# A first pair of sequences with a stream of its own: loads in order of use, offset sums on VectorE, second places for q and k, pinned orders

## The chip, the cores and the metric

One core of a Trainium2 chip. The metric is device microseconds of one execution; smaller is better. All times below are microseconds (us) unless marked otherwise, counted in the profile from the start of the span.

## The reference

Two transformer layers over x of shape (16, 256, 512) with a context of the same shape, 16 heads of 32.

```python
# layer 0: cross attention with a mask, then a GELU MLP
xq, ctx = layer_norm(x, qn_w, qn_b), layer_norm(context, cn_w, cn_b)
q, (k, v) = xq @ q_w, split(ctx @ kv_w)
attn = softmax(where(xa_mask, -max, q @ k.T / sqrt(32)))
x = x + (attn @ v) @ proj_w + proj_b
x = x + gelu(layer_norm(x, n2_w, n2_b) @ fc1_w + fc1_b) @ fc2_w + fc2_b
# layer 1: causal self attention, cross attention, a ReLU MLP, each with a residual and a layer norm
```

The change is in the start of layer 0's attention.

## The kernel before

The 16 sequences are taken as 8 pairs (`NB = 2`, `NG = 8`); a pair has 512 rows, `G = 4` tiles of 128. Matrix products run in float32r, and each operand is held as a high part and a rest, so a product is three matrix instructions (`mm3`).

`phase1` is layer 0's attention. For each pair, `feed(g)` makes the inputs of attention: `normal` loads a tile of x or of the context and normalises it (statistics on VectorE, a power on GpSimd, scaling on VectorE); `transposed` turns it on TensorE and `split` writes high part (ScalarE) and rest (VectorE) into `x_t` or `c_t`; `project_t` makes q and k, four column blocks each with 12 instructions of 512 columns; `values` makes v. `att.stream` is the attention itself: scores (`ps_s`), mask and minimum, exponential, transposes, product with v.

The norms' gain and offset are folded into the weights. `Weight.load` fetches a 128x512 piece into a staging tile `wst` and writes gain times piece, high part on ScalarE (L193) and rest on VectorE (L194). `weigh` (from L216) sums offset times piece over the four pieces into `by_k`: the first on GpSimd (L220), the others scaled on ScalarE (L222) and added on GpSimd (L223). `shift` makes the bias from that sum with matrix products against ones (`ps_b`, L230) and copies it (L231). The splits of q and k (L122, L123) need this bias. `load_o` does the same for the output weight, whose offset is v's bias.

`att.keep` stores a q or k tile to DRAM scratch (`d<-qk`), and `build` loads head stacks from there (`stack<-d`). There is one place for a q tile and one for a k tile (`halves`, `bufs=1`), so a split waits for the store before it.

`weave` interleaves attention with `feed`. In the first round attention only marks its start, so `feed(0)` runs alone: the first scores come when all of it has been put on TensorE. After that `feed(1)` and later ones run beside the attention of the pair before.

TensorE's instructions keep the program's order (`manual_schedule` on PE). For ScalarE, VectorE, GpSimd and SyncE (which issues all transfers) a planner chooses the order, by simulated costs, when the program is built; on the chip each engine then runs its list in order.

Of the kernel before, what the change touches and what calls it, by code (L numbers as in the profile page):

```python
# [2 lines left out]

# [7 lines left out]
F32 = mybir.dt.float32  # L11
# [30 lines left out]
def kernel(ctx: ExitStack, tc: tile.TileContext, a, out):  # L42
# [72 lines left out]
    def bcast(dram_row, n):  # L115
        return dram_row.to_broadcast([P, n])


    def split(src, dst, bias=None, scale=None):

        if bias is not None:
            nc.scalar.activation(dst[0], src, AF.Identity, bias=bias)  # L122
            nc.vector.scalar_tensor_tensor(  # L123
                dst[1], src, bias, dst[0].bitcast(F32), ALU.add, ALU.subtract
            )
        elif scale is not None:
            nc.scalar.activation(dst[0], src, AF.Copy, scale=scale)
            nc.vector.scalar_tensor_tensor(  # L128
                dst[1], src, scale, dst[0].bitcast(F32), ALU.mult, ALU.subtract
            )  # L130
        else:
            nc.scalar.copy(dst[0], src)
            nc.vector.tensor_tensor(dst[1], src, dst[0].bitcast(F32), ALU.subtract)

    def split_sb(src, dst):
        nc.vector.tensor_copy(dst[0], src)
# [7 lines left out]
    class Weight:  # L144
# [29 lines left out]

        def load(self, ks, x0=0, n=C):

            at = slice(x0, x0 + n)
            for k in ks:
                h, l = self.w[0][:, k, at], self.w[1][:, k, at]
                raw = self.stage()  # L180
                nc.sync.dma_start(
                    out=raw, in_=a[self.name][ts(k, P), self.c0 + x0 : self.c0 + x0 + n]
                )
                self.raw[k] = raw
                if self.gain is None:
                    if self.pooled:
                        nc.gpsimd.tensor_copy(h, raw)
                    else:
                        nc.scalar.copy(h, raw)
                    nc.gpsimd.tensor_tensor(out=l, in0=raw, in1=h.bitcast(F32), op=ALU.subtract)  # L190
                else:
                    by = self.gain[:, k : k + 1]
                    nc.scalar.activation(h, raw, AF.Identity, scale=by)  # L193
                    nc.vector.scalar_tensor_tensor(  # L194
                        l, raw, by, h.bitcast(F32), ALU.mult, ALU.subtract
                    )
        def weigh(self, pool):

            self.by_k = None
            for k, raw in self.raw.items():  # L200
                self.by_k = weigh(pool, self.by_k, raw, self.offset[:, k : k + 1])

        def shift(self):
            by_k = self.by_k
# [8 lines left out]
        w.load(range(KC))  # L213
        return w

    def weigh(pool, total, raw, offset):  # L216

        if total is None:
            total = pool.tile([P, 512], F32, tag="xr", name="by_k", bufs=3)
            nc.gpsimd.tensor_scalar(total, raw, offset, None, ALU.mult)  # L220
        else:
            nc.scalar.activation(raw, raw, AF.Identity, scale=offset)  # L222
            nc.gpsimd.tensor_tensor(out=total, in0=total, in1=raw, op=ALU.add)  # L223
        return total

    def sum_cols(b, by_k):

        ps = bank("mm", "ps_b")
        for c in range(4):
            nc.tensor.matmul(ps[:, c : c + 1], by_k[:, ts(c, P)], ones, start=True, stop=True)  # L230
        nc.vector.tensor_copy(b, ps[:, 0:4])  # L231
# [312 lines left out]
    def values(pool, w, src, v, tiles, between=()):  # L544
        for t in tiles:
            ps = yield from project(w, src, t)
            vt = pool.tile([P, C], F32, tag="v", name="v", bufs=6)
            nc.scalar.copy(vt, ps)
            v.append(vt)
            if t - tiles[0] < len(between):  # L550
                yield between[t - tiles[0]]()


    def phase1():
# [7 lines left out]
        att = Attention(pool, scratch, 3, False)  # L562
        w = {}

        def stage():
            return pool.tile([P, C], F32, tag="pts", name="wst", bufs=6)

        def load(n):
            by, off = (cvec[:, x, :] for x in ((0, 1) if n == "q" else (2, 3)))
            w[n] = load_weight(  # L570
                wqkv,
                stage,
                "q_w" if n == "q" else "kv_w",
                KC,
                C,
                C if n == "v" else 0,
                by,
                off,
                "col",
                wo,  # L580
            )
            w[n].weigh(wo)

        def load_o():
            w["o"] = load_weight(wo, stage, "proj_w", KC, C, form="row")
            w["b_o"] = wo.tile([P, C], F32, name="b_o")
            nc.sync.dma_start(out=w["b_o"], in_=bcast(a["proj_b"], C))

            w["o"].offset = w["v"].b
            w["o"].weigh(wo)  # L590
# [5 lines left out]
        class Block0(Job):  # L596
# [5 lines left out]
                    self.shared = (HPC - 1,)  # L602

            def begin(self):
                if self.g == 0:
                    self.load_mask()
                    for t in range(G):
                        self.mask(t)
                if self.g + 1 < NG:
                    after = jobs[self.g + 1]  # L610
                    after.load_mask()
                    att.later += [lambda t=t: after.mask(t) for t in range(G)]
# [38 lines left out]
        jobs = [Block0(g) for g in range(NG)]  # L651
        inputs = {}

        def normal(g, tag, t):
            x = ins.tile([P, C], F32, tag="xin", name="xin", bufs=4)
            nc.sync.dma_start(out=x, in_=of({"x_t": "x", "c_t": "ctx"}[tag], g)[:, t, :])
            normalize(pool, x, x)
            return x

        def front(g, tag, t, x=None):  # L660
            def go():
# [6 lines left out]
        def residual_row(g, at, xr=None):  # L668
            if xr is None:
                xr = wo.tile([P, C], F32, tag="xr", name="xr", bufs=3)  # L670
            nc.sync.dma_start(out=xr, in_=of("x", g)[:, at, :])
            nc.gpsimd.tensor_tensor(out=xr, in0=xr, in1=w["b_o"], op=ALU.add)
            return xr

        def turned(n):
            while att.done < n * KC:
                yield None

        def residual(g, i, xrs=None):
            yield from turned(g * NB + i + 1)  # L680
            for t in range(NT):
# [3 lines left out]
                nc.vector.tensor_tensor(xr, ps, xr, ALU.add)  # L685
                nc.sync.dma_start(out=xd[0][g][ts(at, P), :], in_=xr)

        def feed(g):
            if g >= 1:
                yield from more_values(g - 1)  # L690
            if g >= 2:
                yield from residual(g - 2, 1)
            if g < NG:
                job = jobs[g]
                if g == 0:
                    ready = [normal(g, "x_t", t) for t in range(G)]
                    nc.sync.dma_start(out=cvec, in_=a["attn_vec"])
                    nc.sync.dma_start(out=n2, in_=a["mlp_vec"])
                    nc.sync.dma_start(out=b_fc1, in_=a["fc1_b"])
                    load("q")  # L700
                    for t in range(G):
                        yield front(g, "x_t", t, ready[t])()
                for c in range(KC):
                    ps = yield from project_t(w["q"].w, c, inputs["x_t"])
                    if g == 0 and c == 0:
                        w["q"].shift()
                    q, hl = halves(ins, 0)
                    split(ps, hl, w["q"].b[:, c : c + 1])
                    att.keep(job, c, 0, q)
                    for t in FRONTS[c]:  # L710
                        yield front(g, "c_t", t)()
                if g == 1:
                    shift_o()
                if g == 0:
                    load("k")
                for c in range(KC):
                    ps = yield from project_t(w["k"].w, c, inputs["c_t"])
                    if g == 0 and c == 0:
                        w["k"].shift()
                    k, hl = halves(ins, 1)  # L720
                    split(ps, hl, w["k"].b[:, c : c + 1])
                    att.keep(job, c, 1, k)
                    if g + 1 < NG:
                        for t in FRONTS[c]:
                            yield front(g + 1, "x_t", t)()
                if g == 0:
                    load("v")
                yield from values(pool, w["v"].w, inputs["c_t"], job.v, range(NT))
                if g == 0:
                    w["v"].shift()  # L730
                    load_o()
            if g >= 1:
                yield from residual(g - 1, 0)

        def more_values(g):

# [15 lines left out]

        main = att.stream(jobs)
        for r in range(NG):
            weave(main, Attention.COST, feed(r), (16 * 12 + 8) * PASS)
        weave(main, Attention.COST, last(), (6 * 12 + 32) * PASS)
        left.close()
        return w["mlp"]
# [869 lines left out]
```

## Time and profile before

| | |
|---|---|
| median of 3 runs | 2765.36 us (2759.3 to 2766.42) |
| the profiled execution | 2762.91 us, its span 2761.2 us |
| TensorE busy | 2657.0 us (96%) |
| VectorE busy | 2051.9 us (74%) |
| ScalarE busy | 1821.9 us (66%) |
| GpSimd busy | 630.3 us (23%) |
| first scores product on TensorE | 70.25 us |

Busy times of different engines overlap. Where an engine is named PE, PEld, DVE, ACT, POOL or SP, it is TensorE's products, its weight loads, VectorE, ScalarE, GpSimd or SyncE. In a list of waits the columns are: who waited, for whom, total us, times, longest. In a list of groups they are: line, engine, operation, output from inputs, shapes and count, then busy us and mean ns of one, then the idle time before them. The granted clock is TensorE's, 1.00 at full speed; the record has no entry before its first change, and reads 1.00 there.

### The profile page before, as it was taken

Reading aid. Unit: us, or ns where it says so; the run is one execution under the profiler, and the core shown is the slowest. Engines: PE = TensorE matmul, PEld = TensorE weight load, DVE = VectorE, ACT = ScalarE, POOL = GpSimd, SP = SyncE. Lnnn points to the kernel's source line nnn. Section 1 sums busy time; section 2 is a strip of 40 time slices with the busy share of each in tenths; the row PEclk is TensorE's granted clock in tenths of the full one; section 3 lists DMA queues with packets and bytes.
Section 4 is the critical chain, followed back from the end, with each engine's and each line's share of the span. In section 5 each row is a group of like instructions: output and inputs, shape, how many; then the busy total and the mean of one; then the engine's idle time right before and its main releaser. Section 6 shows DMA issues by size and latency. Waiting matters only on the chain.

```text
span 2761.2 us, 56625 instructions
## 1 busy us (share of the span) xinstructions
PE 2657.0 (96%) x18970; PEld 2241.7 (81%) x18970; DVE 2051.9 (74%) x5947; ACT 1821.9 (66%) x5286; POOL 630.3 (23%) x696
## 2 busy tenths in 40 slices
PE   6999999999899998999989999999999999999998
PEld 5777777776899998999968777777777777777787
DVE  7766667657955569999957777777777777777887
ACT  4877777777655555444547778786777776777522
POOL 6222212113401100111211111115212221214333
PEclk9999999999999999999999999999999999999999
DMA  6655656656333344443464665667565665655321
GB/s 214 197 183 170 182 171 192 182 164 169 107 123 138 123 150 175 168 157 136 167 225 159 195 197 187 194 190 227 183 196 188 188 194 170 189 174 173 97 91 54
DMA packets 287808, 465.40 MB, mean 169 GB/s; under 512 B 36256, under 2 KB 188320, under 8 KB 279328
## 3 DMA queue, kind: packets, MB, share of 16 engines
q1 hardware_dynamic: 287520, 461.78, 52.0%
q8 instruction: 153, 2.51, 0.4%
q14 instruction: 135, 1.11, 0.1%
HBM read 284.97 MB, written 176.69 MB: 167 GB/s over the span
## 4 chain that ended last, share of the span: by engine, by line
PE 76%; DVE 10%; DMA 4%; ACT 3%; issue 3%; POOL 2%; SPq 1%; POOLq 0%; DVEq 0%; ACTq 0%
PE ps_p L258 18%; PE ps_v L258 14%; PE down L1027 9%; PE ps_pt L449 9%; PE ps_z L468 5%; PE ps_s L408 5%; PE up_sc L914 5%; PE up_pt L914 3%; PE up_mm L914 3%; PE ps_t L277 2%; DVE e L423 1%; ACT e L433 1%; DVE x L252 1%; DMA d<-qk 1%; PE ps_z L1347 1%
## 5 line engine op out<-in xcount | busy, mean ns | idle before, releaser
L433 ACT ACTIVATE e<-e,mn 128x256 f32<-128x256 f32 (+1 forms) x1024 | 487.5, 480 | 71.7 <-DVE mn L423 69.4
L455 ACT COPY pt<-ps_pt 128x512 f32<-128x512 f32 (+1 forms) x696 | 378.3, 546 | 178.5 <-PE ps_pt L449 165.5
L449 PE MATMUL ps_pt<-ident,e 128*128 128x128 f32 x2816 | 436.3, 273 | 15.4 <-DVE lbias L1289 8.8
L449 PEld LDWEIGHTS ps_pt<-ident,e 128*128 128x128 f32 x2816 | 336.3, 140 | 56.3 <-DVE lbias L1289 5.7
L408 PE MATMUL ps_s<-stack 97*128 97x256 f32 (+1 forms) x1536 | 331.8, 297 | 18.8 <-ACT e L433 12.0
L408 PEld LDWEIGHTS ps_s<-stack 97*128 97x128 f32 (+1 forms) x1536 | 269.0, 190 | 78.3 <-ACT e L433 19.2
L433 ACT ACTIVATE e<-ps_s,mn 128x256 f32<-128x256 f32 x512 | 240.9, 483 | 59.2 <-DVE mn L419 44.0
L1356 POOL TENSOR_TENSOR x<-x,zz 128x256 f32<-128x256 f32 x128 | 95.4, 745 | 737.0 <-DVE zz L1349 687.0
L1027 PE MATMUL down<-w_h,c_t 128*128 128x256 f32 x900 | 255.4, 285 | 5.6 <-DVE c_t L142 5.6
L1027 PE MATMUL down<-w_h,x_t 128*128 128x256 f32 x868 | 245.9, 283 | 4.4 <-ACT x_t L141 4.4
L423 DVE CUSTOM_DVE_ANT_0 e<-mb,ps_s 128x256 f32<-128x256 bf16 x512 | 192.7, 415 | 75.4 <-PE ps_s L408 73.8
L1027 PE MATMUL down<-w_l,x_t 128*128 128x256 f32 x868 | 246.2, 284 | 0.0
L242 POOL TENSOR_TENSOR rstd<-rstd,nhalf 128x1 f32<-128x1 f32 x192 | 142.4, 747 | 360.6 <-DVE rstd L241 358.8
L258 PE MATMUL ps_p<-x_t,q_h 128*128 128x512 f32 x640 | 215.4, 417 | 4.2 <-DVE qk L128 2.1
L419 DVE TENSOR_REDUCE mn<-ps_s 128x2 f32<-128x512 f32 x256 | 175.1, 684 | 48.7 <-PE ps_s L408 46.5
L468 PE MATMUL ps_z<-pt,v 128*32 128x256 f32 (+1 forms) x3072 | 202.2, 370 | 7.2 <-DVE pt L453 6.5
L423 DVE CUSTOM_DVE_ANT_0 e<-tri,ps_s 128x128 f32<-128x128 f32 (+1 forms) x512 | 160.2, 346 | 53.6 <-PE ps_s L408 51.3
L433 ACT ACTIVATION_READ_ACCUMULATOR e<-e,mn 128x1 f32 x1024 | 197.5, 193 | 0.0
L1027 PEld LDWEIGHTS down<-w_h,c_t 128*128 128x128 f32 x900 | 171.0, 190 | 7.8 <-DVE c_t L142 7.8
L1027 PEld LDWEIGHTS down<-w_h,x_t 128*128 128x128 f32 x868 | 166.4, 192 | 4.8 <-ACT x_t L141 4.6
L468 PEld LDWEIGHTS ps_z<-pt,v 128*32 128x32 f32 x3072 | 83.5, 109 | 105.8 <-issue 28.0
L1027 PEld LDWEIGHTS down<-w_l,x_t 128*128 128x128 f32 x868 | 165.2, 190 | 0.0
(250 smaller groups left out, 7247.8 us busy)
## 6 DMA issues: line engine op xcount, KB each, us to landing
stack<-d SPq DMA_DIRECT2D x1152, 128.0 KB
d<-qk SPq DMA_DIRECT2D x192, 512.0 KB
hid<-ho SPq DMA_DIRECT2D x32, 1024.0 KB
raw<-hid SPq DMA_DIRECT2D x32, 1024.0 KB
x<-xd SPq DMA_DIRECT2D x128, 256.0 KB
xd<-x SPq DMA_DIRECT2D x96, 256.0 KB
xin<-in_x_dram SPq DMA_DIRECT2D x32, 256.0 KB
xin<-in_ctx_dram SPq DMA_DIRECT2D x32, 256.0 KB
```

Source lines behind the costliest of these rows:

```text
L242: nc.gpsimd.tensor_tensor(out=rstd[:, 1:2], in0=rstd[:, 0:1], in1=nhalf, op=ALU.pow)
L258: nc.tensor.matmul(ps, w[p], x[q], start=(k == 0 and i == 0), stop=(k == kc - 1 and i == 2))
L408: nc.tensor.matmul(ps[:, t, :], u.st[: self.rows, 0, j, ts(t, P)], u.st[: self.rows, 1, j, :], start=True, stop=True,)
L419: nc.vector.tensor_reduce(mn, ps, AX.X, ALU.min)
L423: nc.vector.tensor_tensor_reduce(out=e[:, at], in0=bias[t], in1=ps[:, t, : job.width[t]], scale=-SC, scalar=BIG, op0=ALU.add, op1=ALU.min, ...
L433: nc.scalar.activation(e[:, at], ps[:, t, :] if bias is None else e[:, at], AF.Exp, bias=mn[:, t : t + 1], scale=-1.0, accum_out=u.rs[:, t ...
L449: nc.tensor.transpose(pp[:, ts(x, P)], e[:, at : at + P], ident)
L455: nc.scalar.copy(pt[:, :n], pp[:, :n])
L468: nc.tensor.matmul(z[ts(j, D), w[0] * P :], job.v[u.i * NT + mc][:, u.c * P + j * D : u.c * P + (j + 1) * D], u.pt[j][:, x0 * P : (x0 + le ...
L914: nc.tensor.matmul(ps[:, mm, :], w[p][:, k, :], x[q][:, k, :], start=(first and mm == k == j == 0), stop=(k == 1 and j == 2), skip_group_c ...
L1027: nc.tensor.matmul(ps[:, t, :], x[p][:, mm, ts(t, P)], w[r][:, bo, :], start=(q == mm == t == j == 0), stop=(q == self.NS - 1 and mm == 1 ...
L1356: nc.gpsimd.tensor_tensor(out=xv, in0=xv, in1=zz, op=ALU.add)
```

## The change

The first pair leaves `feed` and gets `first()`, woven in the same place.

- `first_loads` issues, as one block in program order on SyncE: x of the first pair, the norm vectors, q's pieces, the context, k's pieces, three of v's, the mask, x of the second pair, v's fourth piece. `Weight.load` is divided into `fetch` and `part`. Staging takes the 6 places of `pts` and, for five pieces, those of the exponentials `e`; the context is loaded into places of v.
- 40 transposes of the identity with itself are put on TensorE ahead, and 5 after each x tile; nothing reads them.
- `weigh` runs on VectorE: one `tensor_scalar` and three `scalar_tensor_tensor`, each multiply and add. This holds for the output weight too.
- Column blocks 1 to 3 of q and k of the first pair are written to places of `z_t` instead of the single q or k place.
- `behind(...)` pins what a block issues on an engine behind a given instruction of that engine.
- The first mask is converted on ScalarE, after k's last split; the output weight is loaded and converted behind v's copies; `n2` and `b_fc1` are loaded there too. The bias product uses a `pt` bank in place of an `mm` bank. Residual rows of pair 0 keep the program's order.

```diff
+        def fetch(self, k, x0=0, n=C):
+            self.raw[k] = self.stage()
+            nc.sync.dma_start(
+                out=self.raw[k], in_=a[self.name][ts(k, P), self.c0 + x0 : self.c0 + x0 + n]
+            )
+        def part(self, k, x0=0, n=C):
...
+                by = self.gain[:, k : k + 1]
+                nc.scalar.activation(h, raw, AF.Identity, scale=by)
+                latest["w"] = nc.vector.scalar_tensor_tensor(
+                    l, raw, by, h.bitcast(F32), ALU.mult, ALU.subtract
                 )
+        def weigh(self, pool):
+            self.by_k = pool.tile([P, 512], F32, tag="xr", name="by_k", bufs=3)
+            for k, raw in self.raw.items():
+                by = self.offset[:, k : k + 1]
+                if k == 0:
+                    nc.vector.tensor_scalar(self.by_k, raw, by, None, ALU.mult)
                 else:
+                    last = nc.vector.scalar_tensor_tensor(
+                        self.by_k, raw, by, self.by_k, ALU.mult, ALU.add
                     )
+            return last
...
-        if total is None:
-            total = pool.tile([P, 512], F32, tag="xr", name="by_k", bufs=3)
-            nc.gpsimd.tensor_scalar(total, raw, offset, None, ALU.mult)
-        else:
-            nc.scalar.activation(raw, raw, AF.Identity, scale=offset)
-            nc.gpsimd.tensor_tensor(out=total, in0=total, in1=raw, op=ALU.add)
...
-        ps = bank("mm", "ps_b")
+        ps = bank("pt", "ps_b")
...
+        def behind(those):
+            with ExitStack() as stack:
+                for x in those:
+                    stack.enter_context(tc.issue_after(x))
+                yield
+        places = iter([("pts", 6)] * 6 + [("e", 5)] * 5)
...
+            nc.sync.dma_start(out=n2, in_=a["mlp_vec"])
+            nc.sync.dma_start(out=b_fc1, in_=a["fc1_b"])
...
+        def first_loads():
+            for t in range(G):
+                fetched[0, "x_t", t] = fetch(0, "x_t", t)
+            nc.sync.dma_start(out=cvec, in_=a["attn_vec"])
+            for n in "qkv":
+                weight(n)
+            for k in range(KC):
+                w["q"].fetch(k)
+            for t in range(G):
+                fetched[0, "c_t", t] = fetch(0, "c_t", t)
+            for n in "kv":
+                for k in range(KC):
+                    if n == "k" or k < 3:
+                        w[n].fetch(k)
+            jobs[0].load_mask()
+            for t in range(G):
+                fetched[1, "x_t", t] = fetch(1, "x_t", t)
+            w["v"].fetch(3)
...
+            if g == 0:
+                tc.keep_in_program_order(load)
...
+        turns = itertools.cycle((0, 1))
+        def spare_halves(slot):
+            tag = f"z_t{next(turns)}"
+            t = wo.tile([P, KC, S], F32R, tag=tag, name=f"qk{slot}", bufs=2)
...
+        def first():
+            job = jobs[0]
+            idle = bank("z", "ps_w")
+            def turn_nothing(n):
+                for i in range(n):
+                    nc.tensor.transpose(idle[:, ts(i % KC, P)], ident, ident)
+            turn_nothing(40)
+            with tc.manual_schedule(engines={mybir.EngineType.SP}):
+                first_loads()
+            ready = [normal(0, "x_t", t) for t in range(G)]
+            w["q"].part(0)
+            for t in range(G):
+                yield front(0, "x_t", t, ready[t])()
+                turn_nothing(5)
+            with behind((latest["h"].ins, latest["l"].ins)):
+                for k in range(1, KC):
+                    w["q"].part(k)
+            inputs_split, q_rest = latest["h"].ins, latest["w"].ins
+            with behind((q_rest,)):
+                w["q"].weigh(wo)
+            def keep(n, slot, c, ps):
+                t, hl = (spare_halves if c else lambda slot: halves(ins, slot))(slot)
+                split(ps, hl, w[n].b[:, c : c + 1])
+                att.keep(job, c, slot, t)
+            for c in range(KC):
+                ps = yield from project_t(w["q"].w, c, inputs["x_t"])
+                if c == 0:
+                    ps0 = ps
+                    continue
+                if c == 1:
+                    w["q"].shift()
+                    keep("q", 0, 0, ps0)
+                keep("q", 0, c, ps)
+                if c == 1:
+                    with behind((inputs_split, latest["l"].ins)):
+                        load("k")
+                for t in ((), (), (0, 1, 2), (3,))[c]:
+                    with behind((q_rest,)):
+                        cost = front(0, "c_t", t)()
+                    yield cost
+            context_split = latest["h"].ins, latest["l"].ins
+            with behind(context_split):
+                k_sum = w["k"].weigh(wo).ins
+            for c in range(KC):
+                ps = yield from project_t(w["k"].w, c, inputs["c_t"])
+                if c == 0:
+                    w["k"].shift()
+                    with behind((context_split[0], k_sum)):
+                        load("v")
+                keep("k", 1, c, ps)
+                for t in FRONTS[c]:
+                    with behind(context_split[1:]):
+                        cost = front(1, "x_t", t)()
+                    yield cost
+            with behind((latest["l"].ins,)):
+                w["v"].weigh(wo)
+            yield from values(pool, w["v"].w, inputs["c_t"], job.v, range(NT))
+            with behind((latest["h"].ins,)):
+                for t in range(G):
+                    nc.scalar.activation(job.mb[:, t, :], job.mk[:, t, :], AF.Copy, scale=NEG)
+                w["v"].shift()
+            with behind((latest["v"].ins,)):
+                load_o()
...
-            weave(main, Attention.COST, feed(r), (16 * 12 + 8) * PASS)
+            weave(main, Attention.COST, feed(r) if r else first(), (16 * 12 + 8) * PASS)
```

## The prediction

> **What bounds the kernel now.** The page comes first: TensorE is busy 2657.0 us of 2761.2, so any time in which it has nothing to run is lost from the end. I then asked for the busy time by stretch, cut where the first pair of sequences starts and stops. The first scores matrix product starts at 70.25 (timeline). Columns: length, then busy time (count) of PE, PEld, DVE, ACT and POOL, granted clock, DMA share, GB/s.
>
> ```profile
> 0.00:7.66 7.66, 0.00 (x0) 0.00 (x0) 3.63 (x12) 1.49 (x2) 3.92 (x21) 1.00 0.74 214
> 7.66:19.07 11.41, 4.97 (x17) 3.29 (x17) 10.71 (x22) 9.50 (x16) 10.51 (x9) 1.00 0.86 283
> 19.07:31.13 12.06, 8.62 (x27) 6.51 (x28) 9.75 (x19) 7.00 (x12) 11.71 (x11) 0.81 0.34 103
> 31.13:45.85 14.72, 13.42 (x56) 10.42 (x56) 9.60 (x18) 4.21 (x8) 13.32 (x14) 0.92 0.70 228
> 45.85:52.48 6.63, 2.70 (x17) 2.10 (x17) 4.67 (x9) 3.04 (x5) 1.83 (x2) 0.85 0.45 159
> 52.48:70.25 17.77, 17.77 (x77) 14.56 (x76) 10.66 (x24) 4.77 (x8) 2.19 (x4) 0.86 0.74 254
> ```
>
> PE works 47.47 of these 70.25 us, VectorE 49.02, GpSimd 43.47. After 70.25 PE is busy 2609.51 of 2690.92 (97%). PE's order is written by hand and does not change after the first pair, so I take it that a first scores product that is G us earlier ends the kernel G us earlier. T is the time of that product, 70.25 now. Next, PE's waits before T:
>
> ```profile
> PE ps_t L277 <- DVE xin L247: 11.3, 4, 7.7
> PE ps_b L230 <- POOL by_k L223: 3.2, 1, 3.2
> PE ps_p L258 <- DVE x_t L133: 2.9, 1, 2.9
> PE ps_b L230 <- DVE qk L123: 1.9, 1, 1.9
> ```
>
> The first is mostly the load of x (7.7); the others are the offset sums on GpSimd and VectorE working on other things first. The chain of waits adds a transfer and shows matrix products at two speeds:
>
> ```profile
> 39.51 6.51 DMA d<-qk
> 46.11 0.70 ACT qk L122
> ...
> 52.69 5.04 PE ps_p L258 x12
> ...
> 64.19 5.44 PE ps_v L258 x24
> ```
>
> There is one place for q, so the next split waits for the store. Twelve products take 5.04 at the half clock (0.42 each), 24 take 5.44 at the full one (0.227). Last, the prices (groups before 70.3):
>
> ```profile
> L223 POOL TENSOR_TENSOR by_k<-by_k,wst 128x512 f32<-128x512 f32 x9 | 12.2, 1361 | 0.2
> L247 DVE TENSOR_SCALAR xin<-xin,mv,rstd 128x512 f32<-128x512 f32 x16 | 11.9, 751 | 1.5 <-POOL rstd L242 1.4
> L194 DVE SCALAR_TENSOR_TENSOR kv_w_l<-wst,cvec,kv_w_h 128x512 fp32r<-128x512 f32 x8 | 8.9, 1124 | 1.6 <-ACT kv_w_h L193 1.6
> L194 DVE SCALAR_TENSOR_TENSOR q_w_l<-wst,cvec,q_w_h 128x512 fp32r<-128x512 f32 x4 | 3.0, 743 | 0.7 <-ACT q_w_h L193 0.7
> ```
>
> The same L194 instruction costs 0.743 for q and 1.124 for k and v, and L247 varies from 0.54 to 1.54, where GpSimd runs offset sums and mask conversions beside it.
>
> **The floor of the new start.** PE: 120 products x 0.227 = 27.2, 12 x 4 transposes x 0.11 = 5.3 (the chain has four in 0.44), three bias products x 0.9 = 2.7: 35.2, after x at 7.7. VectorE: 12 normalisations x 1.43 (0.69 + 0.10 + 0.10 + 0.54, by start times) = 17.2; 12 weight parts x 0.743 = 8.9; 12 splits x 0.68 = 8.2; 8 q/k splits x 0.75 = 6.0; and the offset sums that come to it, 3 x (0.53 + 3 x 0.74) = 8.3. Together 48.6 from 3.5 on. The scale-only step takes 0.53 as L247 does alone; the multiply-add has two SBUF inputs as L194 has, so 0.74 and at worst 1.12. No row has that operation on VectorE; the worst adds 9 x 0.38 = 3.4, and below 0.53 nothing speaks for a gain. So VectorE is the tight engine, and no T under 53 is to be had.
>
> **Part by part, along VectorE and PE.**
>
> *Loads.* Five of SP's issue groups are put in one order: about 29 issues of 0.4 us, 6.6 MB. At the 283 GB/s of the second stretch that is 23 us: q by 8 to 10, context by 15, k by 19, v by 22. None is used earlier than that. Two of them wait in SP's queue, the next pair's x for places that x frees (12 to 18), v's last piece for q's first raw piece (after q's sum, 18). Behind them stand the stores of q, which start at 21 at the earliest: cost 0; without that cover each us would delay stack loads that have some 25 us of slack before T.
>
> *Idle transposes.* 40 start at 1.75, when the identity is ready (POOL, 1.41 + 0.29). At the half clock one takes 0.22 (eight in 1.97), at the full one 0.11. PE's clock changes in steps of 3.41 us in this trace (to half at 26.58, full at 33.41, half at 50.48, full at 57.31). On that grid one step ends at 6.1, so 20 run slowly, 20 fast, and they end at 8.3, when x is there. The last x tile is transposed by 11.8, 4 x 5 idle ones between; its split ends at 13.2.
>
> *q.* Its other three parts are pinned behind that split; VectorE ends the last at 15.5, PE's first column block at 16.1, the second at 18.9. The sum runs 15.5 to 18.2, so the bias product (18.9 to 19.9) no longer waits, which removes the 3.2. The split places remove the 6.51 store from the chain; six of the eight q and k tiles get spare ones.
>
> *Context.* The four normalisations follow the q sum: VectorE has 5.7 for them, 3.0 for q splits, 2.7 for context splits, 3.0 for k parts, 14.4 from 18.2: last context split at 32.5, since k parts and q splits share the queue. PE would be ready at 30: a new wait of 2.5, VectorE's.
>
> *k.* First block 32.5 to 35.3; k's sum is pinned behind the context splits and ends at 36.0; bias 37.0. Then v's parts (3.0) stand ahead of the next pair's x normalisations in program order, so PE, which wants their transposes next, gets the first at 41.5: a wait of 4.5 that the change makes. From there three blocks 8.3, four sets of transposes 1.8 with 2.2 of waits for their normalisations, v's two blocks 5.5, v's bias 1.0: T = 41.5 + 18.8 = 60.3. If the planner places part of the normalisations ahead of v's parts, 2 us less. I take **T = 59.3**, G = 11.0.
>
> *After T.* Mask conversion on ScalarE: 4 x 0.48 (nearest row: L433, 128x256), beside v's products: 0. The output weight's conversion moves behind v's copies, 4 x 0.61 = 2.45 on ScalarE's queue, ahead of exponentials; the three L222 at 70.71 (1.95) are gone: +0.5. Its sum, 2.8 on VectorE, where 70.25 to 80 has 5.59 of 9.75 busy: hidden, 2.8 if not.
>
> Sum: -11.0 + 0.5 = -10.5. The profiled execution took 2762.91 (span 2761.2), so 2752.4; the median shown is 2.45 above it, so 2754.9. A measurement here tells 0.3% from nothing, 8.3 us.
>
> **Does an idle transpose raise the clock?** These stretches are the clock's own steps:
>
> ```profile
> 26.58:30.00 3.42, 3.08 (x13) 2.68 (x14) 2.19 (x4) 1.71 (x4) 3.21 (x4) 0.50 0.20 79
> 30.00:33.41 3.41, 3.14 (x9) 2.28 (x9) 1.78 (x3) 2.55 (x5) 3.27 (x5) 0.50 0.58 172
> 50.48:53.90 3.42, 2.69 (x10) 1.89 (x9) 2.98 (x5) 2.00 (x4) 0.10 (x1) 0.50 0.41 126
> ```
>
> The first, 90% busy with bias products and transposes, did not bring the full clock; the second, 0.86 of transposes and the rest wide products, did; the third, 1.48 of transposes and 1.4 of products, did not. No step here is filled by transposes alone, so it stays open. The Trainium skill, "TensorE: Matmul & The Clock Gate", Part 4: PE-mode transpose, says that transposes do not count as busy for the clock, which speaks against this part. By that rule the first row is as it should be, and the sum would be that of the first rival.
>
> **Rivals.**
>
> 1. *The clock stays at half through the transposes.* 40 x 0.215 = 8.6 end at 10.4; four sets of nine at 1.93 end at 18.1; the last split at 18.3 instead of 13.2, and all that is pinned behind it 5 later. T = 64.3, gain 5.5: 2759.9, no difference. For it the row at 26.58; against it that wide products could be what lacked there. 0.20.
>
> 2. *VectorE's pinned queue has holes.* T = 3.5 + 48.6/u + 1.0 at a busy share u. T = 59.3 needs 0.89. VectorE's share from 3.5 to 70.25 is 0.73 now; at that T = 71, time 2767, no difference. It turns slower below 0.66. Against it: the waits in those stretches are for GpSimd, stores and loads, which the change takes away. 0.04 within 0.3%, 0.04 slower.
>
> 3. *The rest is planned anew, for the worse.* ScalarE, VectorE, GpSimd and SP run in an order that a planner lays out from its own costs, and the start feeds into it. PE idles 81.4 us after T, in places such as 2.54 at 658.7 behind VectorE's pt. If that grows by over 18.8 us (23%) the kernel is slower; at 25%, +20.4, 2775.3. Against it: neighbouring 100 us stretches of one kind differ by under 2 us. Slower, 0.08.
>
> 4. *The planner fills the two new waits* (2.5 and 4.5), T = 53 to 54, VectorE's floor: gain up to 16.5, 2749. Against it: no stretch above has VectorE without holes. 0.10.
>
> **How the numbers follow.** The forecast, 2754.9, has 0.54. Faster: 0.54 + 0.10 = 0.64; same: 0.20 + 0.04 = 0.24; slower: 0.04 + 0.08 = 0.12. The range goes down to 2745.5, rival 4 less 3.5 us of spread between executions (the runs shown lie up to 6.1 under their median), and up to 2767, which takes in rival 1 and the no-gain end of rival 2; the slower cases, 0.12, are left out. The forecast's own range is 2750 to 2757.
>
> **What would show it.** The first scores product near 59; wide products at 0.23 from the first on (right) or transposes at 0.22 to 12 and beyond (rival 1); the q bias product with no wait for the sum; PE's waits before T led by VectorE's normalisations near 25 to 32 and 37 to 42; no wait of the q and k splits (L122 now) for d<-qk. PE's idle time after T, 81.4 now, would show rival 3. The prediction is wrong if T falls by 9 or more and the end does not.

## The result, and the profile after

The changed kernel takes 2742.9 us (median of 6 runs, 2737.32 to 2745.44), the kernel before 2763.47 (6 runs, 2759.3 to 2767.84): a ratio of 0.9921 [0.9907, 0.9936], 20.6 us less. The forecast was 2754.9 with a range from 2745.5; the gain was nearly twice the 10.5 forecast, and the time lies 2.6 us below the range. The profiled execution took 2743.56 us, its span is 2741.8.

T, the start of the first scores product, went from 70.25 to 62.71: a gain of 7.5, where 11.0 was forecast. The other 12 us came after T, where the sum had a loss of 0.5. The busy time by stretch after the change (columns as before: length, busy time and count of PE, PEld, DVE, ACT and POOL, granted clock, DMA share, GB/s):

```profile
0.00:7.66 7.66, 5.92 (x40) 5.74 (x40) 3.53 (x11) 1.49 (x2) 3.91 (x21) 1.00 0.72 236
...
25.10:38.80 13.70, 9.27 (x45) 6.72 (x43) 11.15 (x23) 5.85 (x10) 1.09 (x2) 1.00 0.73 240
38.80:49.04 10.24, 8.22 (x26) 6.82 (x27) 8.96 (x24) 1.75 (x3) 2.33 (x4) 0.50 0.32 103
49.04:62.71 13.67, 13.39 (x67) 10.89 (x66) 9.45 (x18) 5.98 (x13) 1.10 (x2) 1.00 0.69 233
62.71:2741.80 2679.09, 2607.86 (x18780) 2206.26 (x18779) 2001.46 (x5852) 1793.37 (x5237) 590.31 (x641) 0.99 0.53 168
```

Read the last row first. PE does the same 18,780 products as before after T, with 1.65 us less busy time (2607.86 against 2609.51), but it is idle for 71.2 us there instead of 81.4. This idle time was the sign that the prediction named for its third rival; it moved the other way. The row from 38.80 holds a surprise of the start: the granted clock is half for 10.24 us.

PE's waits before T in the changed kernel (who waited, for whom, total, times, longest):

```profile
PE ps_b L236 <- DVE by_k L214: 4.0, 3, 2.2
...
PE ps_t L283 <- DVE xin L253: 1.2, 1, 1.2
```

The 11.3 us for normalised tiles fell to 1.2, the 3.2 for GpSimd's sums are gone; what leads now are the bias products, which wait for VectorE's sums (1.5 for q, 2.2 for k). The prices of VectorE in the start (groups of instructions: busy us and mean ns of one, then idle time before):

```profile
L214 DVE SCALAR_TENSOR_TENSOR by_k<-wst,cvec,by_k 128x512 f32<-128x512 f32 x9 | 6.6, 737 | 0.1
L253 DVE TENSOR_SCALAR xin<-xin,mv,rstd 128x512 f32<-128x512 f32 x12 | 6.4, 537 | 1.8 <-POOL rstd L248 1.7
L202 DVE SCALAR_TENSOR_TENSOR kv_w_l<-wst,cvec,kv_w_h 128x512 fp32r<-128x512 f32 x8 | 5.5, 744 | 0.0
```

An add is 0.737, a weight part of k and v 0.744 (1.124 before), a scaling 0.537 (0.751 before): every one costs about what its cheapest row of before cost. The waits after T show where part of the 12 us was; this line of the kernel before

```profile
PE ps_s L408 <- ACT e L433: 12.0, 16, 3.0
```

has become, in the changed kernel,

```profile
PE ps_s L414 <- ACT e L439: 6.6, 15, 0.7
```

No such wait is longer than 0.7 in this profile. (In a second profile of each kernel it is 15.5 with a longest of 3.2 before, and 10.4 with a longest of 1.5 after.) Yet from 165 us on ScalarE, GpSimd and SP run the same lists in the same order in both kernels, and VectorE too but for one exchange near 1080 us: hardly anything was planned anew there.

### The profile page after: what moved, and what is told of

Read it like the earlier page. It is cut to its first block, busy times and chain, and to the rows that moved or that the text cites. A ratio compares the mean times of both kernels' runs of the same rounds, so it can differ in the third digit from the quotient of the medians.

```text
span 2741.8 us, 56705 instructions
## 1 busy us (share of the span) xinstructions
PE 2659.8 (97%) x19030; PEld 2248.4 (82%) x19030; DVE 2050.6 (75%) x5963; ACT 1817.0 (66%) x5278; POOL 602.3 (22%) x676
## 3 DMA queue, kind: packets, MB, share of 16 engines
q8 instruction: 153, 2.51, 0.4%
## 4 chain that ended last, share of the span: by engine, by line
PE 77%; DVE 11%; DMA 5%; issue 3%; ACT 2%; POOL 1%; SPq 1%; POOLq 0%; DVEq 0%; ACTq 0%
PE ps_p L264 18%; PE ps_v L264 14%; PE down L1138 10%; PE ps_pt L455 9%; PE ps_s L414 5%; PE ps_z L474 5%; PE up_sc L1025 5%; PE up_pt L1025 3%; PE up_mm L1025 3%; PE ps_t L283 2%; DMA d<-qk 1%; DVE e L429 1%; ACT e L439 1%; DVE x L258 1%; DVE st L244 1%
## 5 line engine op out<-in xcount | busy, mean ns | idle before, releaser
L414 PE MATMUL ps_s<-stack 97*128 97x256 f32 (+1 forms) x1536 | 332.6, 298 | 13.1 <-ACT e L439 6.6
```

What stands on the lines that cost most here:

```text
L414: nc.tensor.matmul(ps[:, t, :], u.st[: self.rows, 0, j, ts(t, P)], u.st[: self.rows, 1, j, :], start=True, stop=True,)
```

## The experiments

Twelve kernels ran, four at a time; each batch has its own runs of the kernel before on the same chip (medians 2769.69, 2763.81, 2769.28), so ratios are compared. In the table "T" is from one profiled execution; "idle after T" is PE's idle time from T to the end there; "rest" is the gain in the ratio, times 2765, less what T gained against 70.0 (mean of two profiles of the kernel before, 70.28 and 69.66, by the instruction's own start).

| kernel | idle transposes | T | idle after T | ratio to before | rest |
|---|---|---|---|---|---|
| before, run again | 0 | 69.66 | 88.3 | 1.0005 [0.9995, 1.0015] | -1.7 |
| before + 60 idle | 60 | 68.12 | 73.3 | 0.9948 [0.9936, 0.9961] | 12.5 |
| before + 128 idle | 128 | 73.74 | 89.5 | 1.0015 [1.0004, 1.0025] | -0.4 |
| after (first runs) | 60 | 62.71 | 71.2 | 0.9921 [0.9907, 0.9936] | 14.6 |
| after, run again | 60 | 64.48 | 78.5 | 0.9933 [0.9914, 0.9951] | 13.0 |
| after, no idle ones | 0 | 62.47 | 84.7 | 0.9964 [0.9950, 0.9979] | 2.4 |
| after, 128 idle | 128 | 69.48 | 76.8 | 0.9983 [0.9973, 0.9994] | 4.2 |
| after, 30 idle | 30 | 63.48 | 75.0 | 0.9929 [0.9915, 0.9943] | 13.1 |
| after, one place for q and k | 60 | 69.92 | 72.4 | 0.9960 [0.9947, 0.9973] | 11.0 |
| after, sums on GpSimd | 60 | 65.76 | 77.3 | 0.9955 [0.9943, 0.9968] | 8.2 |
| after, no pins | 60 | 71.01 | 69.6 | 0.9945 [0.9932, 0.9957] | 16.2 |
| after, clock held, 60 idle | 60 | 63.95 | 75.0 | 0.9929 [0.9914, 0.9944] | 13.6 |
| after, clock held, 90 idle | 90 | 62.37 | 77.4 | 0.9950 [0.9934, 0.9965] | 6.2 |

### First batch: both kernels again, and two parts undone

The two kernels once more, unchanged:

> The kernel before, unchanged, profiled a second time. Theory 1 (the 12 us gained after the first scores product lie in places where one execution differs from the next): its first scores product is at 70.25 again within 0.5 us, but its TensorE waits after that differ from the first profile by 5 us and more in sum, in places such as the context load at 2301. Theory 2 (the change shortens those waits for good): they repeat within 2 us.

> The changed kernel, unchanged, profiled a second time. Theory 1: first scores product at 62.7, the lead over the kernel before at the end anywhere between 8 and 20 us in its profile. Theory 2: the lead grows from 7.8 to 19 between 600 and 2500 us again, in the same places (680, 1400, 1800 to 1920, 2090, 2310).

The totals came as before (2770.87 and 2750.51 us), the gain after T too. The waits of one execution are not those of the next, though: after T PE idles 6.9 us more in the second profile of the kernel before, and 7.3 more in that of the changed kernel, so they do not repeat within the 2 us of theory 2. The lead of the changed kernel does grow again, by 11.3 us between 600 and 2500 us (12.0 the first time), though not at 680. A difference of 7 us between two single profiles therefore says little; the ratios rest on 4 to 19 runs of each kernel.

Without the idle transposes:

```diff
-            turn_nothing(40)
...
-                turn_nothing(5)
```

> The changed kernel without the 60 idle transposes. If they raise the clock, the first products of q run at 0.42 instead of 0.23 for some 5 us: first scores product 1 to 3 us later than 62.7, the time 1 to 3 us more. If they do not, or if VectorE sets the pace there anyway, no later than 63, and x's transposes start no earlier.

T did not move (62.47), but the kernel took 2757.78 us, 7.3 more than the changed kernel beside it. So the idle transposes do nothing for T and yet are worth most of the gain after it. The lists of the other engines are the same in both but for two exchanges before 16 us, so the planner has no part in this.

One place each for q and k again:

```diff
-                t, hl = (spare_halves if c else lambda slot: halves(ins, slot))(slot)
+                t, hl = halves(ins, slot)
```

> The changed kernel with one place each for q and k of the first pair, as before. If the store of q was on the path, each split waits some 4 to 6 us for the store ahead of it: first scores product 6 to 10 us later (69 to 73) and the time as much more. If VectorE's queue sets the pace alone, under 2 us.

T 69.92, total 2757.54: 5.4 to 7.2 later by T, 7.0 in the total. Its chain of waits (start, length, what) has the stores that the prediction took out, with the next split right behind, as here:

```profile
32.39 4.10 DMA d<-qk
...
36.60 0.70 ACT qk L125
```

The gain after T stayed (11.0), so the stores have no part in that.

### Second batch: is it the length of TensorE's program?

The theory by then: the page of every kernel lists a queue that carries instructions, in the kernel before

```profile
q8 instruction: 153, 2.51, 0.4%
```

(queue, kind: packets, MB, share). 2.51 MB in 153 packets is 16.4 KB each, and the changed kernel's 19,030 products and as many weight loads on TensorE make about 249 instructions to a packet: TensorE's program, brought in piece by piece. The trace of the kernel before bears this out. With its semaphore waits counted in, TensorE starts 255.8 instructions on average between the starts of two packets, and each of the 153 starts when this count, divided by 256, leaves between 144 and 255. Sixty transposes are 120 of its instructions. They shift by half a packet the places of the work at which every later packet comes.

Only the idle transposes, in the kernel before:

```diff
+            turn_nothing(40)
...
+                turn_nothing(5)
```

> The kernel before with nothing but the 60 idle transposes (40 at the start, 5 after each x tile), which lengthen TensorE's program by 120 instructions. Fetch theory (the gain after T comes from where the 16 KB packets of TensorE's program fall among SyncE's issues, and 120 instructions move every later packet): T stays at 68 to 71, PE's time from T to the end falls by 5 to 12 us against before, the total is 6 to 14 us shorter; waits ps_pt for lbias after T 7 in place of 10 or 11. Rival (the time after T belongs to another part of the change, such as the later store traffic or the output weight): total within the change of T, so 0 to 2 us shorter, with 10 or 11 waits for lbias. By the prediction's step on the clock alone: T earlier by at most 2 us, since q's products here wait for x and the weights.

2748.14 us, 0.9948, with T only 1.9 earlier: 60 transposes that compute nothing give the old kernel two thirds to three quarters of the whole change's gain, somewhat more than the 6 to 14 us expected. The waits for lbias went from 10 to 7, as expected. The planner laid out the start of the other engines a little differently here (up to 70 us); after that their lists are those of the kernel before but for one exchange on VectorE at 704 us.

The changed kernel with 128 idle ones, one packet more than none:

```diff
-            turn_nothing(40)
+            turn_nothing(108)
```

> The kernel after with 108 idle transposes at the start in place of 40: TensorE's program is 256 instructions, one 16 KB packet, longer than without any idle ones, so later packets fall in the same places of the work as in a_no_idle. They end near 15 us in place of 6, so T is 6 to 9 us later. Fetch theory: PE's time from T to the end is as in a_no_idle, 5 to 12 us longer than in after; the total is 12 to 20 us longer than after, about the time of before. Rival (idle transposes help by something else than the phase): time from T to the end as in after, the total 6 to 9 us longer than after.

T 69.48; the rest of the gain is 4.2 in place of 13.0 to 14.6, near the 2.4 without any. By the ratios the total is 13.8 to 17.1 us longer than after's (0.9983 against 0.9933 and 0.9921), in the 12 to 20 expected. PE's idle time in its one profile (76.8) does not show it, though: it lies between the two profiles of after.

The offset sums back on GpSimd and ScalarE (the pin behind k's sum becomes one behind the context's splits):

```diff
-                    nc.vector.tensor_scalar(self.by_k, raw, by, None, ALU.mult)
+                    nc.gpsimd.tensor_scalar(self.by_k, raw, by, None, ALU.mult)
...
-                    last = nc.vector.scalar_tensor_tensor(
-                        self.by_k, raw, by, self.by_k, ALU.mult, ALU.add
-                    )
+                    nc.scalar.activation(raw, raw, AF.Identity, scale=by)
+                    nc.gpsimd.tensor_tensor(out=self.by_k, in0=self.by_k, in1=raw, op=ALU.add)
```

> The kernel after with the offset sums back on GpSimd and ScalarE (the pins kept but for the one to k's sum). If VectorE is the tight engine of the start, as forecast, it loses 8 us of work before T, but the sum takes 1.36 an add and slows VectorE beside it: T between 2 earlier and 6 later, I take 4 later (the q bias product waits 2 to 3, k's 2 more). Total by the same amount: 0 to 6 longer than after. Time from T to the end as in after, since TensorE's program has the same length.

T 65.76, 1.3 to 3.1 later than after; the total 6 to 9 longer by the ratios, with intervals of 4. PE waits 7.0 for the sums (longest 4.4) in place of 4.0. With the sums there, a weight part of k and v on VectorE takes 0.886 and a scaling 0.693, against 0.744 and 0.537 in after and 1.124 and 0.751 before: so the sums on GpSimd made up a part of the old prices. The gain after T is 8.2 here, where it was expected as in after, since TensorE's program is as long; with intervals of this size that may be chance, and it stays open.

The pins taken away:

```diff
             with ExitStack() as stack:
                 for x in those:
-                    stack.enter_context(tc.issue_after(x))
+                    pass
                 yield
```

> The kernel after with the pins of behind(...) taken away (the planner may put weight parts and sums where it likes). If the pins matter: x's splits or the context's come behind weight parts, T 3 to 8 us later, and the total by the same. If the planner would choose nearly the same order: T within 1.5 us, the total within 3. Time from T to the end as in after, since TensorE's program has the same length.

T 71.01, 6.5 to 8.3 later: PE waits once 5.7 us for a split of x and once 4.9 for one of q or k, where the longest such wait in after was 1.1. The total is only 3 to 7 us longer than after. The pins are worth as much at T as the second places, and the prediction had no price for them.

### Third batch: a whole packet, a quarter, and the clock

The kernel before with 128 idle transposes (108 at the start):

```diff
+            turn_nothing(108)
...
+                turn_nothing(5)
```

> The kernel before with 128 idle transposes (108 at the start, 5 after each x tile): 256 instructions, one whole packet, where b_idle_only had 120. Fetch theory: the gain goes again; T 68 to 74 (the idle ones end near 16 us), PE's time from T to the end within 3 us of before, total within 5 us of before plus T's change. Rival (idle transposes help by themselves, by the clock or by the time at which the first pair ends): 12 to 16 us shorter than before, as b_idle_only was, plus T's change.

2773.02 us, 3.7 more than the kernel before, and T is 3.7 later: all of the gain is gone. Sixty of them help, 128 do not: it is not the idling, but where it leaves the rest of the program. The two kernels side by side, PE's stretch from T to the end, 60 first:

```profile
68.12:2746.60 2678.48, 2605.14 (x18780) 2203.64 (x18779) 2002.12 (x5849) 1792.64 (x5238) 587.11 (x637) 0.99 0.53 168
```

```profile
73.74:2776.80 2703.06, 2613.57 (x18780) 2206.70 (x18779) 2006.03 (x5849) 1793.24 (x5238) 587.23 (x637) 0.99 0.53 167
```

The same products, 24.6 us apart in these two executions, 16.2 of it idle time. The profiled execution with 128 is the longest of its eleven, 5.5 us above their median, so the distance is shown too large; for the same reason the stretch is 4.6 and 12.1 us longer than in the two profiles of the kernel before, where 3 was expected.

Thirty idle ones, in the changed kernel:

```diff
-            turn_nothing(40)
+            turn_nothing(10)
```

> The kernel after with 30 idle transposes in place of 60 (10 at the start): its later packets lie a quarter of a packet off both a_no_idle and after. T at 62 to 64.5 as in both. Fetch theory: a time between 2743 and 2758 by which places are hit (no order of size is foreseen); the waits of PE after T stand where a packet falls on one of SP's issues 8 to 10 us ahead of them, and nowhere else. Rival (the number does not matter, idle ones at all do): as after, within 2 us.

0.9929: as good as 60. This is what the rival expected (within 2 us of after); the theory of packets had foreseen no size, so this run by itself speaks for the rival, if for either. The runs with 128 speak against it. Only 0, 128 and, in part, 90 idle ones fall where it hurts.

Idle transposes around k's bias product, against the half clock from 38.8:

```diff
+                    turn_nothing(20)
                     w["k"].shift()
+                    turn_nothing(10)
```

> The kernel after with 20 idle transposes ahead of k's bias product and 10 behind it, to keep the clock at full while PE waits for k's sum; 90 idle ones in all. The clock stays at full from 38 to 49 us, where it was at half for 10.2 us: T 2 to 5 earlier than after, 58 to 61. The total: T's gain, and what the shift by 60 instructions does to the waits after T, which may be as large (up to 8 either way). If the granted clock falls in spite of them, T is within 1 us of after.

The same with 10 idle ones at the start instead of 40, 60 in all:

> As x3_warm_k with 10 idle transposes at the start in place of 40, so 60 in all as in after: the later packets fall as in after. T 58 to 61. Fetch theory: PE's time from T to the end as in after (within 4 us), so the total 1 to 6 us shorter than after's, a ratio to before of 0.989 to 0.993. Rival (the phase is not what sets the time after T): the same time from T to the end as x3_warm_k.

A miss for T: 62.37 and 63.95, where 58 to 61 was expected. With 90 the clock fell all the same, to half from 43.93 to 47.34, and T is within 1 us of after's, as expected for that case. With 60 the clock stayed at 1.00 from 32.4 on, but there k's sum came later: its last add starts at 40.56, in the two profiles of after at 38.11 and 39.54. From that add to the next x's transposes it takes 3.9 us in all three, at either clock. From there to T it takes 19.5, against 20.3 to 21.0 in the three profiles with 10.24 us at the half clock (after's two and the one without idle ones). So the half clock had cost 0.8 to 1.5 us, less than expected: VectorE is busy 11.39 of the 12.04 us from 37 to 49 in this kernel, and PE, faster now, waits for it. For the program's length the pair speaks as expected: the same start, 60 against 90 idle ones, 0.9929 against 0.9950, and the rest of the gain is 13.6 and 6.2. No kernel of these is clearly faster than the changed one.

### How a packet costs time: one place in three kernels

Seen in the issues of SP (start, length, line, what) in the kernel before, then with 60 and with 128 idle transposes, at the same two instructions of SP's list:

```profile
1757.64 1.50 SPq L393 DMA_DIRECT2D stack<-d  x1
1759.24 0.38 SPq L378 DMA_DIRECT2D d<-qk  x1
```

```profile
1749.97 0.43 SPq L393 DMA_DIRECT2D stack<-d  x1
1750.50 0.38 SPq L378 DMA_DIRECT2D d<-qk  x1
```

```profile
1769.14 1.54 SPq L393 DMA_DIRECT2D stack<-d  x1
1770.78 0.38 SPq L378 DMA_DIRECT2D d<-qk  x1
```

The same issue takes 1.50, 0.43 and 1.54. In the kernel before, the transfers from 1757.5 to 1759 hold one packet of the instruction queue,

```profile
q8 instruction: 1, 0.02, 4.5%
```

so does the window from 1768.9 to 1770.4 with 128; with 60 the window from 1749.1 to 1750.6 holds none. Eight us on, on PE (start, length, line, what, and in brackets the idle time before), in the same order:

```profile
1765.88 0.52 PE L449 MATMUL ps_pt<-ident,e 128*128 128x128 f32 x3 [0.55 <-DVE lbias L1289]
```

```profile
1757.54 0.49 PE L449 MATMUL ps_pt<-ident,e 128*128 128x128 f32 x3
```

```profile
1777.30 0.52 PE L449 MATMUL ps_pt<-ident,e 128*128 128x128 f32 x3 [0.47 <-DVE lbias L1297]
```

At this place PE waits where the issue was long, and not where it was short. How one leads to the other stands in the chain of waits of the kernel before (start, length, what):

```profile
1761.66 2.73 DMA dbias<-lbias
...
1764.48 0.42 DVE lbias L1288
...
1765.40 0.34 DVE lbias L1289
1765.74 0.14 issue
1765.88 0.52 PE ps_pt L449 x3
```

A small store (`dbias`) goes out behind the head stacks that the long issue delayed. SP's next issue waits 2.4 us for it to land, 1.4 in the kernel with 60 and 2.3 with 128. VectorE's next copy into `lbias` waits for the same landing, and the add behind it (at 1765.40) reads the PSUM bank that PE's next transposes need (both are places of `pt`). So the name in brackets is right. That the delayed head stacks are what holds up the store is read off the order of the issues, and not shown.

Over whole kernels: in before 72 of SP's 2130 issues take more than 0.9 us (a usual one takes 0.42), and 44 of these have a packet of this queue over them, though packets lie over only some 140 of the 2130. With 60 idle ones in the same kernel 72 are long again: it is not their number that differs, but which they are. An issue can also be compared with itself, over fourteen profiles (the table's and the first of the kernel before). From 165 us on 710 issues lie under a packet in some of these and free of it in others: under a packet 585 of 1764 took over 0.9 us, free of it 71 of 8174.

Then I compared the steps from one product's start to the next on PE, product by product and from the same one on (75 to 87 us into the span), over the fourteen profiles. There are 51 places where some kernel's step is over 0.5 us longer than the shortest of all. The excess there adds up to 21.6 to 34.6 us in the five profiles with 0 or 128 idle ones (mean 29.2), to 12.5 to 23.4 in the seven with 60 (mean 17.1). The groups overlap a little, but the difference of their means, 12.1, is about as large as that of the rest of the gain, 10.6 (12.7 on average with 60, 2.1 in the changed kernels and the old one with 0 or 128). Seven of these places, picked afterwards, all in the later attention, hold 5.6 to 10.2 us with 0 or 128 and 0.0 to 2.0 with 60.

How much of this stands behind a packet? Of the 29.2 and the 17.1, 10.5 and 3.2 lie where a long issue under a packet ended 1 to 12 us earlier: 7.2 of the 12.1. But 17% of all products have such an issue ahead of them, and of the steps at these places that are over 0.4 us too long no more than 27%. With 30 idle ones it is 5.3 of 18.5, so the expectation that waits stand there and nowhere else does not hold.

Shown by this: the gain after T depends on the number of instructions ahead, and a whole packet more brings back the time without any, in both kernels (a second period was not run); and an issue of SP is long far more often under a packet than the same issue without one. Followed at one place only: how a long issue becomes a wait of PE. Not shown: that all of the gain comes this way, by what a packet holds up an issue, and why at a third of them and not at the others (the median issue under a packet takes 0.43). No kernel took the packets themselves away.

## Why the prediction was wrong, point by point

**The step that failed** is the cost of the idle transposes. They had one term, the clock at the start; the sum had nothing for the 120 instructions by which they move the rest of TensorE's program. Measured, that is 12.5 us in the kernel before; in the changed one it is 7.3 by the totals and 10.6 by the rest (13.0 against 2.4 without them). It is the larger part of the gain. So the "+0.5" after T became a gain of some 13. The time lies only 12.0 below the forecast because T missed by 3.4 the other way, which is luck. The Trainium skill, "Runtime: NRT & Kernel Launch", Instruction fetch mechanics, says that instructions come in 16 KiB blocks of 256 over DMA and that crossing a block's border is "mostly hidden". The traces agree with the size (16.4 KB, 255.8 instructions) and with the hiding on TensorE itself: over such a border a step on PE is on average some 0.003 us longer than the shortest of the fourteen profiles, as elsewhere. What they add is a price on another engine, in SP's issues, 1.50 in place of 0.43.

**T earlier by G, the end earlier by G** held on average. With 60 or 30 idle ones the four kernels with T from 62.7 to 64.5 have a mean ratio of 0.9928, three with T from 68.1 to 71.0 one of 0.9951: 6.4 us for 6.0 us of T. The kernel with its sums on GpSimd (65.76, 0.9955) lies some 5 us off that line.

**T itself, 59.3 forecast and 62.7 measured, was mis-sized.** In its order:
- The idle transposes do raise the clock. Forty alone on PE, the first eight in 1.70 us, then eleven in 0.90; from start to start they take 0.213 up to 4.58 and 0.109 from 4.72 on (the clock's record begins at 4.64, and the column reads 1.00 ahead of that too):

```profile
1.70:3.40 1.70, 1.66 (x8) 1.66 (x9) 0.00 (x0) 0.57 (x2) 1.65 (x10) 1.00 0.84 266
...
5.10:6.00 0.90, 0.90 (x11) 0.90 (x9) 0.17 (x2) 0.00 (x0) 0.56 (x1) 1.00 0.98 306
```

  So the first rival's mechanism is out. The rule of the Trainium skill, "TensorE: Matmul & The Clock Gate", Part 4: PE-mode transpose, that transposes do not engage the full clock, does not hold here (0.213, then 0.109). But the price of this clock was wrong too: without any idle ones, eight transposes of x take 1.97 at the half clock and T is the same, since x's transposes wait for loads and normalisation, and q's products find the full clock at 13.8 anyway.
- q's start came as forecast (first products at 0.23 each from 13.96). Its bias product still waits, 1.5, now for VectorE.
- The store no longer holds up the splits. That is worth 5.4 to 7.2 us of T, against 6.51 in the chain of before: right.
- The last context split came at 33.8 (forecast 32.5), k's sum at 38.8 (36.0, where 32.5 and the sum's own 2.75 give 35.3): the planner put four statistics of the next pair's x among its adds. The next x's transposes came at 42.0 (41.5).
- From there to T 20.7 in place of 18.8. One block of k ran at half clock (5.03 for twelve products, the next 2.76); with the clock held this stretch took 19.5. So about 1 of the 1.9 is the half clock, which the sum did not have here.
- Over the whole start VectorE is busy 48.99 us, against 48.6 forecast, in the 59.2 from 3.5 to T, a share of 0.83; the forecast needed 0.89. The work was right, the holes were under-sized. (The second rival's formula gives 63.1 at 0.83, but this share is taken from the measured T, so that is no test of it.) That VectorE is not alone in setting T shows in the last 13.67 us, where PE is busy 13.39.
- Loads at no cost, mask conversion hidden (4 in 1.32), the sums at 0.737 each: right.

**The rivals.** The third had the right place (PE's idle time after T) with the wrong cause and sign. The fourth, T of 53 to 54, did not come, though the time went below its 2749.

## What to carry to other kernels

When a change adds or removes instructions on an engine with a long straight program, it shifts all later instruction packets against the work; here, with transfers issued just in time, that alone moved the end by half a per cent. Before crediting a small gain to what the edit was meant to do, run the old kernel with nothing but as many idle instructions added, and once more with a whole packet of them. And price a shorter start by a range of the tight engine's busy share: here it was 0.73 before, 0.89 in the forecast and 0.83 in the end.

## What the runs showed of the hardware that I had not expected

TensorE's program comes in packets of 16.4 KB, one for every 256 of its instructions, 153 of them in the kernel before. The same SP issues took over 0.9 us in 585 of 1764 cases under such a packet and in 71 of 8174 without one. At one place an issue took 1.50 us instead of 0.43, and 8 us later PE stopped for 0.55 us, by way of a small store and an add on VectorE. Idle transposes of 128x128 raised the clock by themselves, in after's two profiles 2.9 and 5.7 us after the first of them; and a clock at half for 10.24 us cost only 0.8 to 1.5 us, because the engine that PE waits for was no faster.
